# A graph network on sparse lists: the stage that builds the lists, from the scheduler's order to an order written by hand

## The chip, the core and the metric

The kernel runs on one core of a Trainium2 chip, in one launch. The metric is the device time of that launch in microseconds (us). A core has five engines that work at once, each with its own in-order queue of instructions: TensorE (PE; its weight loads are shown as PEld), VectorE (DVE), ScalarE (ACT), GpSimd (POOL) and SyncE (SP). SP only starts DMAs here; POOL also starts the gathers. Semaphores order the engines among each other.

## What is computed

Two residual layers of graph attention on 4096 nodes of 512 features. The adjacency is a 4096 x 4096 matrix of zeros and ones whose density falls with both the row and the column number, so that the first rows have many neighbours and the later ones few. Cut to what matters:

```python
x = layernorm(x + gat0(x, adj, W, a))                # 8 heads of 64
def gat(x, adj, W, a):                               # per head
    h = x @ W
    e = leaky_relu(h @ a_dst + (h @ a_src)[None], 0.2)   # N x N
    e = where(adj > 0, e, -inf)
    return softmax(e) @ h
h1 = elu(gat(x, adj, W1, a1))                        # 8 heads of 64
h2 = elu(gat(h1, adj, Wo, ao))                       # 1 head of 512
x = layernorm(x + relu(h2 @ lin1_w + lin1_b) @ lin2_w + lin2_b)
```

## The kernel before, in words

The kernel never forms the N x N scores. In a first stage, the graph stage, it turns each tile of 128 rows of the adjacency into a list of edges (source node in `idx`, target row in `nl`), 128 edges to a chunk, 927 chunks in all. Three attention layers then gather the projected rows of the listed nodes from a table in memory and sum them. If a list did not fit its room, a flag would start a dense path that is not run with these inputs. The change is in the graph stage alone, which `find_edges` issues and which also computes the first projection.

There are 35 lists. Rows 0 to 127 (tile 0) have so many edges that they make four lists, by column ranges; tiles 1 to 31 make one each. `parts()` gives for each list the room per row `k`, the number of chunks `n` and the segments of columns within which at most 8 (tile 0: 24) neighbours are looked for. A list goes this way:

- SP loads the adjacency rows (`raw`, int32), ACT turns them into bf16 zeros and ones (`sg`), and PE adds a multiple of the column number to each edge by two matmuls per 512 columns (`key`, in PSUM, two buffers of 1024 columns).
- DVE takes the eight largest keys of each segment (`cand`, MAX8; for tile 0 three rounds with a replacement between), then the `k` largest of the candidates (`lst`) in rounds of MAX8 and MATCH_REPLACE8. Each round needs the one before it.
- ACT makes column numbers of them (`qs`) and the row's degree (`signs`, `balance`); POOL makes `degs` and `counts`.
- PE sums the counts over the rows (`prs`, one PSUM bank). ACT makes from it where each row starts and ends and compares that with a ramp (`starts`, `ends`, `sides`), and POOL adds the two halves into `s1`, the matrix that spreads rows over edges. ACT and POOL split the columns into two bf16 parts (`rhs`, `rest`).
- PE multiplies `s1` with those parts (`pl`, one PSUM bank, in up to four pieces); ACT copies `nl`; DVE picks each edge's column (`sel`, `src`); POOL writes `hole` and `idx`.

Beside it, for each of 32 node tiles, `x` is loaded (`xr`), turned by PE (`pt`), copied by ACT (`xt`), multiplied with the weights in two halves of eight fp32 matmuls in all (two passes each, `ph`), and copied into a row of the table (`hrow`), which SP writes. `load_projection` loads the weights of a layer and adds columns `w @ a` to them: POOL multiplies (`sprod`), DVE sums.

In the code the lists come by tile number. `places_of` delays the second half of a list's way (`place`) by one list, and `beside(t)` issues one projection after each tile. But this stage is not under `tc.manual_schedule()`: a scheduler takes the instructions and orders each engine's queue anew, by its own idea of costs. The attention layers that follow are under `manual_schedule` and keep the order in which the code issues them. Their first gathers wait for the whole table and for `idx`.

Of the kernel before, what the change touches and what calls it, by code (L numbers as in the profile page):

```python
# [10 lines left out]
F32 = mybir.dt.float32  # L11
# [547 lines left out]
def sparse_path(  # L559
# [84 lines left out]
    def load_projection(pool, st, w, a):  # L644

        hs, dm = st.heads, st.dim


        st.w = pool.tile([P, FC, 2, st.wide], F32, name=f"sw_{st.name}")
        for c in range(FC):  # L650
            for j in range(2):
                mine = st.w[:, c, j, :HF]
                if hs > 1:
                    nc.sync.dma_start(
                        mine.rearrange("p (k o) -> p k o", o=dm),
                        w[ts(j, hs // 2), ts(c, P), :].rearrange("k f o -> f k o"),
                    )
                else:
                    nc.sync.dma_start(mine, w[0, ts(c, P), ts(j, HF)])
        with tc.tile_pool(name=f"swload_{st.name}", bufs=2) as wp:  # L660
            for side in range(2):
                ab = wp.tile([P, hs, dm], F32, name="sab")
                nc.sync.dma_start(ab, a[:, ts(side, dm)].partition_broadcast(P))
                d = (side == 1) == st.dest_first
                for c in range(FC):
                    prod = wp.tile([P, 2, HF], F32, name="sprod")
                    nc.gpsimd.tensor_mul(  # L667
                        prod, st.w[:, c, :, :HF], ab.rearrange("p h d -> p (h d)").rearrange("p (j f) -> p j f", j=2)
                    )
                    if hs > 1:  # L670
                        at = HF if d else HF + hs // 2
                        nc.vector.tensor_reduce(
                            st.w[:, c, :, at : at + hs // 2],
                            prod.rearrange("p j (h d) -> p j h d", d=dm), AX.X, OP.add,
                        )
                    else:
                        nc.vector.tensor_reduce(st.w[:, c, int(d), HF:], prod, AX.XY, OP.add)
# [12 lines left out]

    def project_in(ps, st, columns, n=P):

        halves = []
        for j in range(2):
            ph = ps.tile([P, st.wide], F32, name="ph")
            for c in range(FC):
                nc.tensor.matmul(ph[:n], columns(c), st.w[:, c, j], start=(c == 0), stop=(c == FC - 1))  # L697
            halves.append(ph)
        return halves
# [73 lines left out]
    def edge_constants(big):  # L773
# [64 lines left out]
        return frac, places, iota_e, iota_k, row1, own_b, before, values, mids, ends_at, by_parts  # L838

    def signs_of(sb, t, pieces=1):  # L840

        raw = sb.tile([P, N], I32, name="raw", bufs=2)
        sg = sb.tile([P, N], BF16, name="sg")
        w = N // pieces
        for i in range(pieces):
            nc.sync.dma_start(raw[:, ts(i, w)], adj[ts(t, P), ts(i, w)])
        for i in range(pieces):
            nc.scalar.activation(sg[:, ts(i, w)], raw[:, ts(i, w)], AF.Sign)  # L848
        return sg

    def find_edges(big, sb, ps, pk, constants, sg, beside):

        frac, places, iota_e, iota_k, row1, own_b, before, (less, under), mids, ends_at, by_parts = constants
# [8 lines left out]
        places_of = []  # L864
        for v, p in enumerate(pts):
            t, k, c0, nch = p.t, p.k, p.first, p.n
            if t > 0:
                sg = signs_of(sb, t)
            size = sum(8 * r for _, _, r in p.segs)
            cand = sb.tile([P, size], F32, name="cand", bufs=1 if t == 0 else 2, tag="cand0" if t == 0 else "cand")  # L870
            at = 0
            for w0_ in range(p.lo // 1024 * 1024, p.hi, 1024):
                a, b = max(w0_, p.lo), min(w0_ + 1024, p.hi)
                key = pk.tile([P, 1024], F32, name="key")
                for j in [a] + list(range((a // KW + 1) * KW, b, KW)):
                    e, w = min(b, (j // KW + 1) * KW), j // KW
                    out_ = key[:, j - w0_ : e - w0_]
                    nc.tensor.matmul(out_, ident_b, sg[:, j:e], start=True, stop=False)  # L878
                    nc.tensor.matmul(out_, places[:, w], frac[:, j - w * KW : e - w * KW], start=False, stop=True)  # L879
                for j, n, r in p.segs:  # L880
                    if not a <= j < b:
                        continue
                    part = key[:, j - w0_ : j - w0_ + n]
                    for i in range(r):
                        nc.vector.max(out=cand[:, at : at + 8], in_=part)  # L885
                        if i < r - 1:
                            left = sb.tile([P, 256], F32, name="left")[:, :n]
                            nc.vector.match_replace(
                                out=left, in_to_replace=cand[:, at : at + 8], in_values=part, imm_value=-1.0
                            )  # L890
                            part = left
                        at += 8

            r8 = 8 * p.segs[0][2]
            skip = sum(n <= r8 for _, n, _ in p.segs)
            last = cand.rearrange("p (s e) -> p s e", e=r8)[:, skip:, r8 - 1]
            nc.vector.tensor_reduce(over[:, 0, v : v + 1], last, AX.X, OP.max)
            lst = sb.tile([P, kmax], F32, name="lst")[:, :k]
            for i in range(k // 8):
                nc.vector.max(out=lst[:, ts(i, 8)], in_=cand)  # L900
                if i < k // 8 - 1:
                    nc.vector.match_replace(  # L902
                        out=cand, in_to_replace=lst[:, ts(i, 8)], in_values=cand, imm_value=-1.0
                    )

            qs = sb.tile([P, kmax + 1], F32, name="qs")[:, : k + 1]
# [13 lines left out]
            if p.last:  # L920
                mean = sb.tile([P, 3], F32, name="mean_of")
                nc.gpsimd.tensor_scalar(mean[:, 0:1], sum_, 0.5, None, op0=OP.is_lt)
                nc.gpsimd.tensor_scalar(mean[:, 1:2], sum_, 0.5, None, op0=OP.is_gt)
# [3 lines left out]
                nc.gpsimd.tensor_add(counts[:, v : v + 1], deg, mean[:, 0:1])  # L927
            else:
                nc.gpsimd.tensor_copy(counts[:, v : v + 1], deg)
            deg = counts[:, v : v + 1]  # L930
            def place(v=v, p=p, k=k, c0=c0, nch=nch, qs=qs, deg=deg):
                prs = ps.tile([P, 1], F32, name="prs", tag="small")
                nc.tensor.matmul(prs, before, deg, start=True, stop=True)
                nc.scalar.activation(qs[:, k:], prs, AF.Identity, bias=ends_at[:, v : v + 1], scale=-1.0)

                lim = sb.tile([P, 1], F32, name="lim")
                nc.gpsimd.tensor_sub(lim, deg, mids[:, v : v + 1])
                first = starts[:, v : v + 1]
                nc.scalar.activation(first, prs, AF.Identity, bias=mids[:, v : v + 1], scale=-1.0)
                nc.scalar.activation(ends[:, v : v + 1], prs, AF.Identity, bias=lim)  # L940
                wide = p.blocks * P
                here = s1[:, p.at * P : p.at * P + wide]
                sides = sb.tile([P, 2, most * P], BF16, name="sides")[:, :, :wide]
                nc.scalar.activation(sides[:, 0], iota_e[:, :wide], AF.Sign, bias=first)
                nc.scalar.activation(sides[:, 1], iota_e[:, :wide], AF.Sign, bias=ends[:, v : v + 1], scale=-1.0)  # L945
                nc.gpsimd.tensor_add(here, sides[:, 0], sides[:, 1])  # L946


                rhs = sb.tile([P, 2 * (kmax + 2)], BF16, name="rhs")[:, : 2 * (k + 2)].rearrange("p (h w) -> p h w", h=2)
                rest = sb.tile([P, 2 * (kmax + 1)], BF16, name="rest")[:, : 2 * (k + 1)].rearrange("p (h w) -> p h w", h=2)  # L950
                q2 = sb.tile([P, 2 * (kmax + 1)], F32, name="q2")[:, : 2 * (k + 1)].rearrange("p (h w) -> p h w", h=2)
                shape = [P, 2, k + 1]
                for h in range(2):
                    nc.scalar.activation(rhs[:, h, : k + 1], qs, AF.Copy, scale=half[:, h : h + 1])
                nc.gpsimd.tensor_mul(q2, qs[:, None, :].to_broadcast(shape), half[:, :, None].to_broadcast(shape))
# [44 lines left out]
            if len(places_of) > 1:  # L1000
                places_of.pop(0)()
# [629 lines left out]
```

## Time and profile before

| | us |
|---|---|
| three runs | 2115.8, 2120.51, 2120.89 (median 2120.51) |
| span of the profiled execution, first to last instruction | 2110.3 |
| time around the span, against the median | 10.2 |
| first gather of the first layer (end of the graph stage) | 489.4 |
| busy in 0 to 490: PE, DVE, ACT, POOL | 345.0, 367.1, 294.7, 215.1 |
| busy in the whole span: PE, DVE, ACT, POOL | 1707.7, 1323.1, 663.4, 1155.6 |

The page shows no device time of its own for the profiled execution; its span is compared with spans, and times with times. Busy time is the time in which at least one instruction of the engine ran. Matmuls are pipelined and their shown ends are modelled, so PE's busy time is more than it needs. "A <- B" in a view means that A stood idle until B was done. In a row of the timeline the first number is the start in us from the span's start, the second the duration, and a bracket at the end is the idle time ahead of it and what ended that.

### The profile page before, as it was taken

What the parts mean: (1) busy time and instruction counts of PE and PEld (TensorE: products, weight loads), DVE (VectorE), ACT (ScalarE), POOL (GpSimd) and SP (SyncE); (2) the same over time, 40 slices, a digit from 0 to 9 for tenths busy, and PEclk for the clock granted to TensorE, in tenths of its full rate; (3) what the DMA queues carried; (4) which work ended last, traced back from release to release, by engine and by line L of the source; (5) the groups of instructions that cost most, each with busy time, mean ns of one, the idle gap of its engine ahead of it and who ended that gap; (6) DMA issues with size and microseconds to landing.
All of it is one profiled execution on the core that took longest, in us unless ns stands there. A gap on an engine that the chain in (4) does not pass through costs nothing.

```text
span 2110.3 us, 29302 instructions
## 1 busy us (share of the span) xinstructions
PE 1707.7 (81%) x8987; PEld 999.2 (47%) x8987; DVE 1323.1 (63%) x3933; ACT 663.4 (31%) x2316; POOL 1155.6 (55%) x1658
## 2 busy tenths in 40 slices
PE   4778777663888887848888988579999989998997
PEld 3555443221555565525555665354454444444444
DVE  6887777774899998947878878433433333433412
ACT  3447677664222222202333332121110212111111
POOL 5515444446777777737777777373647444443200
PEclk9899999775899999978999999889999999999999
DMA  7434566634777888737777777373546343534301
GB/s 230 150 101 161 210 259 226 224 145 131 231 234 230 252 238 241 208 87 195 185 189 191 194 200 192 123 223 91 158 119 185 110 127 91 156 103 122 97 13 47
DMA packets 132589, 351.94 MB, mean 167 GB/s; under 512 B 41922, under 2 KB 42954, under 8 KB 128454
## 3 DMA queue, kind: packets, MB, share of 16 engines
q0 software_dynamic: 74160, 206.25, 36.0%
q1 hardware_dynamic: 58262, 143.72, 19.3%
q8 instruction: 74, 1.21, 0.2%
q14 instruction: 93, 0.76, 0.1%
HBM read 347.31 MB, written 42.24 MB: 185 GB/s over the span
## 4 chain that ended last, share of the span: by engine, by line
PE 34%; DVE 19%; issue 15%; POOL 13%; DMA 12%; ACT 6%; SPq 1%; POOLq 0%; DVEq 0%; ACTq 0%
PE acc L1230 11%; PE p L1508 10%; DMA g<-table_t,idx 10%; POOL g L1094 9%; PE ph L697 5%; DVE g L1218 5%; PE p L1520 4%; DVE cand L885 2%; DMA xr<-sx_d 1%; DVE cand L902 1%; POOL s L946 1%; DVE lst L900 1%; ACT sides L945 1%; POOL sprod L667 1%; DVE sm L1197 1%
## 5 line engine op out<-in xcount | busy, mean ns | idle before, releaser
L1094 POOL DMA_INDIRECT g<-table_t,idx x927 | 941.1, 1015 | 552.9 <-issue 232.8
L1230 PE MATMUL acc<-g,sm 128*64 128x260 f32 (+2 forms) x4068 | 580.8, 415 | 175.1 <-DVE g L1218 141.8
L1230 PEld LDWEIGHTS acc<-g,sm 128*64 128x64 f32 x4068 | 328.3, 147 | 391.8 <-DVE g L1218 156.8
L697 PE MATMUL ph<-sw_t,xt 128*128 128x264 f32 (+1 forms) x1536 | 394.0, 404 | 51.5 <-ACT xt L686 51.3
L1218 DVE TENSOR_TENSOR g<-g,wp 128x2048 f32<-128x2048 f32 (+4 forms) x134 | 349.1, 2605 | 6.7 <-ACT wp L1173 6.7
L697 PEld LDWEIGHTS ph<-sw_t,xt 128*128 128x128 f32 x1536 | 291.9, 197 | 120.0 <-ACT xt L686 72.3
L885 DVE MAX8 cand<-key 128x8 f32<-128x353 f32 (+55 forms) x467 | 195.1, 445 | 74.6 <-PE key L879 74.4
L1508 PE MATMUL p<-sht,sl1w 128*128 128x512 f32 (+1 forms) x576 | 228.7, 553 | 0.7 <-DVE xr L1525 0.7
L1520 PE MATMUL p<-sl2w,shid 128*128 128x512 f32 x512 | 226.7, 597 | 0.0
L686 ACT ACTIVATE xt<-pt 128x128 f32<-128x128 f32 x384 | 101.3, 279 | 216.0 <-PE pt L683 215.8
L1508 PEld LDWEIGHTS p<-sht,sl1w 128*128 128x128 f32 x576 | 107.8, 191 | 111.5 <-issue 106.0
L1520 PEld LDWEIGHTS p<-sl2w,shid 128*128 128x128 f32 x512 | 95.2, 190 | 119.9 <-issue 119.4
L1165 DVE TENSOR_TENSOR z<-s,g 128x16 f32<-128x16 f32 (+9 forms) x294 | 46.6, 175 | 138.0 <-DMA g<-table_t,idx 134.9
L878 PE MATMUL key<-sg,s_identb 128*128 128x512 bf16 (+1 forms) x258 | 109.7, 426 | 20.6 <-DVE cand L885 11.1
L1511 ACT ACTIVATE shid<-p,sl1b 128x512 f32<-128x512 f32 (+1 forms) x72 | 46.1, 640 | 242.9 <-PE p L1508 242.9
L1267 DVE SCALAR_TENSOR_TENSOR o<-ex,o 128x512 f32<-128x512 f32 x64 | 44.2, 691 | 124.5 <-ACT ex L1266 124.3
L848 ACT ACTIVATE sg<-raw 128x4096 bf16<-128x4096 int32 (+1 forms) x39 | 116.9, 2996 | 8.9 <-PE key L878 5.2
L710 ACT COPY hrow<-ph 128x260 f32<-128x260 f32 (+2 forms) x194 | 71.0, 374 | 148.8 <-PE ph L697 148.4
L879 PE MATMUL key<-frac,places 128*128 128x512 bf16 (+1 forms) x258 | 109.4, 425 | 2.7 <-POOL places L784 2.7
L1205 DVE TENSOR_SCALAR sm<-iota_n,nl,w 128x64 f32<-128x64 f32 x339 | 83.8, 327 | 30.8 <-ACT w L1176 30.8
L1173 ACT ACTIVATE wp<-z 128x32 f32<-128x32 f32 (+4 forms) x134 | 27.5, 205 | 207.0 <-DVE g L1218 206.5
L1525 DVE TENSOR_TENSOR xr<-p,xr 128x512 f32<-128x512 f32 x32 | 22.0, 688 | 94.1 <-PE p L1520 93.6
(184 smaller groups left out, 1836.8 us busy)
## 6 DMA issues: line engine op xcount, KB each, us to landing
raw<-in_adj_dram SPq DMA_DIRECT2D x31, 2048.0 KB, 7.9
table_t<-hrow SPq DMA_DIRECT2D x64, 260.0 KB, 3.6
xr<-in_x_dram SPq DMA_DIRECT2D x64, 256.0 KB, 4.0
g<-table_t,idx POOLq DMA_INDIRECT x927, 3.8
table_t<-hrow SPq DMA_DIRECT2D x32, 257.0 KB, 4.3
sx_d<-o SPq DMA_DIRECT2D x32, 256.0 KB, 4.6
xr<-sx_d SPq DMA_DIRECT2D x32, 256.0 KB, 4.0
out_dram<-xr SPq DMA_DIRECT2D x32, 256.0 KB, 3.4
```

Of the source, the lines that this page charges most:

```text
L686: nc.scalar.activation(xt[:, c, :], pt[:, c, :], AF.Copy, accum_out=st.xparts[:, c, t : t + 1])
L697: nc.tensor.matmul(ph[:n], columns(c), st.w[:, c, j], start=(c == 0), stop=(c == FC - 1))
L848: nc.scalar.activation(sg[:, ts(i, w)], raw[:, ts(i, w)], AF.Sign)
L878: nc.tensor.matmul(out_, ident_b, sg[:, j:e], start=True, stop=False)
L879: nc.tensor.matmul(out_, places[:, w], frac[:, j - w * KW : e - w * KW], start=False, stop=True)
L885: nc.vector.max(out=cand[:, at : at + 8], in_=part)
L1094: nc.gpsimd.indirect_dma_start(out=u.g[:, k, : self.st.row], out_offset=None, in_=self.st.table[:, :], in_offset=bass.IndirectOffsetOnAxis ...
L1205: nc.vector.tensor_scalar(sm[:, at + i], of_g, node[k], u.w[:, k], op0=OP.is_equal, op1=OP.mult)
L1218: nc.vector.tensor_mul(body, body, wp[:, :, :, None].to_broadcast(body.shape))
L1230: nc.tensor.matmul(out_[g * HN : (g + 1) * HN], sm[:, slot], rows(k), start=start, stop=stop)
L1508: nc.tensor.matmul(p1, l1w[:, c, ts(k, P)], hts[b][:, c, :n], start=(c == 0), stop=(c == FC - 1))
L1520: nc.tensor.matmul(p2, hids[b][:, k, ts(j, P)], l2w[:, k, :], start=(k == 0), stop=(k == HC - 1))
```

## The change

The graph stage gets `tc.manual_schedule()`, and its order is written out:

- A `Clock` counts DVE's time by formulas (`tick`). Steps are put on it with a delay (`later`) and are issued when the count passes their time. `idle` holds work for PE that is issued only while a counter `spare` is positive: it grows with DVE's time and shrinks with PE's work.
- A list's way is cut into `front`, `middle`, `back` and `pick`, each given to the clock by the one before it.
- Lists come by turns: one of the last tile, then one heavy list (tiles 0 to 7) and two light ones from the end.
- The adjacency is loaded and signed in halves of 2048 columns, four buffers each. A load is issued when an earlier half is signed; signs are issued up to four windows of 1024 columns ahead of their use. The very first halves come in four and two pieces.
- Keys of the window after next are issued as soon as DVE is through with a window.
- A projection is three pieces of idle work: the turn and two halves. `load_projection` becomes a generator that gives one product at a time; the weights of the first layer are loaded after the first adjacency halves and multiplied after the first list. Those of the later layers come at lists 14 and 24.
- Some buffers change: `qs`, `rhs`, `rest` three instead of two, `sides`, `sel` and `sab` one instead of two.

The diff, cut to its core:

```diff
+    class Clock:
+        def __init__(self):
+            self.now, self.due, self.count, self.spare, self.idle = 0.0, [], 0, 0.0, []
+        def later(self, delay, fn, *args):
+            self.count += 1
+            heapq.heappush(self.due, (self.now + delay, self.count, fn, args))
+        def tick(self, cost):
+            end = self.now + cost
+            self.spare = min(self.spare + cost, 3.0)
+            while True:
+                if self.due and self.due[0][0] <= end:
...
+                elif self.idle and self.spare > 0 and self.idle[0][0] <= end:
...
+        def drain(self):
+            while self.due or self.idle:
+                self.spare = 1.0
+                self.tick(1.0)
...
+        heavy = [v for v, p in enumerate(pts) if p.t < 8]
+        light = [v for v, p in reversed(list(enumerate(pts))) if p.t >= 8]
+        turns_ = [light.pop(0)]
+        while heavy or light:
+            turns_ += heavy[:1] + light[:2]
+            heavy, light = heavy[1:], light[2:]
...
+        def sign(t, h, pieces=1):
+            raw = raws.pop((t, h))
+            name, bufs = ("sg0", 2) if t == 0 else ("sg", 4)
+            sg = sgs[t, h] = sb.tile([P, HW], BF16, name=name, bufs=bufs)
+            w = HW // pieces
+            for i in range(pieces):
+                nc.scalar.activation(sg[:, ts(i, w)], raw[:, ts(i, w)], AF.Sign)
+            if stream:
+                load(*stream.pop(0))
...
+            clock.later(2.2, middle, v, qs, lim)
+        def middle(v, qs, lim):
...
+            for lo in range(0, p.n, per):
+                clock.later(1.8 + 4.5e-3 * wide, queue, v, rhs, rest, lo, per)
...
+            clock.later(1.6, pick, v, lo, per, pl, kk)
...
+        for j in range(4):
+            load(*stream.pop(0), *cuts[j : j + 1])
+        for j in range(2):
+            sign(*signed.pop(0)[1:], cuts[j])
+        between(-1)
...
+        fill(0)
+        fill(1)
+        for n, v in enumerate(turns_):
...
+            while i < len(windows) and windows[i][0] == v:
...
+                        nc.vector.max(out=cand[:, at : at + 8], in_=part)
+                        tick(0.09 + n_ / 960)
...
+                fill(i + 2)
+                i += 1
+                while signed and signed[0][0] <= i + 3:
+                    sign(*signed.pop(0)[1:])
...
+            front(v, lst)
+            between(n)
+        clock.drain()
...
-        sg0 = signs_of(sb, 0, 8)
-        constants = edge_constants(big)
...
+        pools.enter_context(tc.manual_schedule())
+        constants = edge_constants(big)
+        clock = Clock()
...
+        def turn0(t):
+            xt = turn_in(sb, pp, st0, xrs.pop(t), t)
+            ask0(t + 2)
+            clock.idle.append((clock.now + 2.0, 1.95, half0, (t, xt, 0)))
+        def half0(t, xt, j):
+            ph = project_half(pp, st0, lambda c: xt[:, c, :], j)
+            clock.later(1.5, out0, t, ph, j)
+            if j == 0:
+                clock.idle.append((clock.now + 0.5, 1.95, half0, (t, xt, 1)))
...
+        def between(n):
+            if n < 0:
+                clock.w0 = load_projection(big, sb, st0, w0, a0)
+                first = next(clock.w0)
+                clock.w0 = itertools.chain([first], clock.w0)
+            if n == 0:
+                weigh(clock.w0)
+                clock.later(11.0, ask0, 0)
+                clock.later(11.0, ask0, 1)
+                clock.idle.append((clock.now + 14.0, 0.95, turn0, (0,)))
+            if n == 14:
+                gap[0] = 4.0
+                weigh(load_projection(late, sb, st1, w1, a1))
+            if n == 24:
+                weigh(load_projection(late, sb, st2, wo, ao))
```

## The prediction

> **What bounds the kernel now.** The change touches one stage, so the first question is how long that stage is and what stands still in it. The instructions on `idx` give its end: the layers' first gather starts at 489.4 us of a span of 2110.3. The busy time by stretches says which engine is full up to there; its columns are busy us of PE, PEld, DVE, ACT, POOL with counts in brackets, then granted clock, DMA share, GB/s.
>
> ```profile
> L1094 POOL DMA_INDIRECT g<-table_t,idx x927: 996/1002/1602, 489.4 to 1979.9; - x186
> ```
>
> ```profile
> 300.00:350.00 50.00, 36.82 (x198) 19.48 (x196) 37.79 (x128) 38.03 (x98) 21.19 (x82) 1.00 0.63 229
> ...
> 450.00:490.00 40.00, 21.73 (x109) 9.07 (x107) 26.01 (x89) 19.97 (x49) 17.16 (x68) 0.71 0.06 20
> 0.00:490.00 490.00, 344.97 (x1751) 201.10 (x1751) 367.12 (x1417) 294.74 (x843) 215.10 (x732) 0.89 0.52 184
> ```
>
> No engine is full: DVE, the busiest, works 367 of 490 us. The table of waits within the stage says why: every engine waits for another one's step of a list's way.
>
> ```profile
> DVE cand L885 <- PE key L879: 74.4, 55, 5.7
> ...
> PE prs L933 <- POOL counts L927: 36.0, 29, 3.1
> ...
> PE pl L969 <- POOL s L946: 32.9, 30, 2.1
> ```
>
> The timeline of one light list shows the mechanism. PE reaches the product on `s1` before POOL has made it and stands; the key matmuls for the next list are queued behind; DVE waits for those.
>
> ```profile
> 317.18 0.20 PE L969 MATMUL pl<-rhs,s 128*128 128x52 bf16 x1 [1.66 <-POOL s L946]
> ...
> 318.64 0.22 DVE L885 MAX8 cand<-key 128x8 f32<-128x53 f32 x1 [1.79 <-PE key L879]
> ```
>
> Such a list takes 9.4 us (its `sides` start at 305.19, the next list's at 314.55), of which DVE works 7.1. So the stage is bound by latency in PE's queue, and DVE's own time is what it could shrink to. One more reading decides how far. An instruction of DVE that needs the result of the one just ahead starts after its end; one that needs something older starts before it:
>
> ```profile
> 28.95 0.34 DVE L902 MATCH_REPLACE8 cand<-lst,cand 128x192 f32<-128x192 f32 x1
> 29.33 0.36 DVE L900 MAX8 lst<-cand 128x8 f32<-128x192 f32 x1
> ...
> 461.03 0.44 DVE L885 MAX8 cand<-key 128x8 f32<-128x274 f32 x1
> 461.39 0.22 DVE L900 MAX8 lst<-cand 128x8 f32<-128x72 f32 x1
> ```
>
> 29.33 lies 0.04 after 28.95 + 0.34; 461.39 lies 0.08 before 461.03 + 0.44. Over the stage, 983 of DVE's 1408 neighbouring pairs overlap by 0.083 and 107 stand tight at +0.035: the planner has put another list's work between most dependent steps.
>
> [...] 512-wide key matmuls are 0.43 apart at 459.55 and 0.22 apart elsewhere, with a clock of 0.71 in the last stretch. [...] a sign takes 0.63 for 512 columns and 3.60 for 4096, which leaves 0.2 fixed.
>
> **The change part by part**, S being the time that DVE stands between its first maximum and the end of the last list.
>
> 1. *DVE in hand order: the floor.* The same maxima, replacements and selections are issued (467 + 78 + 161 MAX8, 204 replacements with their value loads, 35 triples and 51 fused selections). But a list's rounds now follow one another with nothing between: the changed program has 498 tight pairs, mostly maximum, replacement, maximum. The durations of all DVE instructions of the stage sum to 448.8. Pairs: 204 value loads overlap by 0.014, 51 accumulator reads by 0.076, 498 stand at +0.035, 655 overlap by 0.083: 448.8 - 2.9 - 3.9 + 17.4 - 54.4 = 405. The same sum for before gives 367, what the table shows. So the hand order costs DVE 38 us, which nothing hides once DVE is the full engine.
> 2. *Start.* The first maximum waits for POOL's `places`, as before (8.32); I take 8.5. The first weights come later: SP now issues eight pieces of adjacency, then two loads that wait until ACT has signed list 31's halves (about 7.6 and 11.6), and only then the eight weight DMAs (6.85 for eight) and the row of `a` (2.63 to land): 11.6 + 6.9 + 0.5 + 2.6 = 21.6 behind 6 MB of adjacency, so some 23. DVE meets the first sum over `sprod` near 18.5 and waits for a product of 1.26: 5 us of S, 1 more for list 31's second half. POOL stands there too, with list 31's `s1` and PE's `pl` behind it.
> 3. *The way in four steps.* `prs` is issued 2.2 us of DVE work after the list, `pl` another 1.8 + 4.5e-3 x width, the selection 1.6 after that. The chain needs about 0.65 on ACT, 0.75 on POOL and 0.4 on PE (1.8); then 0.5 + 1.3 on ACT and 1.2 + 0.3 on POOL (3.3, against 4.1 given at width 512). So PE's waits mostly go, and the 74 us of DVE waiting for keys. What is late next is ACT.
> 4. *Halves on ACT.* 68 signs in place of 39: 62 of 2048 columns at 0.63 + 1536 x 0.83 ns = 1.90, two of 1024 at 1.05, four of 0.63, together 122.4 against 116.9: +5.5. In a light list ACT works 38.03/50 x 9.4 = 7.1 now, 7.3 then; DVE 7.1 plus some seven pairs that become tight at 0.12, about 7.9. ACT at 93% in strict order, with waits for `prs` and `pl` in its queue, will hold DVE up; I take 0.3 for each of 24 light lists, 7 us. The pieces' added DMAs (29 at about 0.33 of SP) lie two tiles ahead, beside other work.
> 5. *Selections and keys.* 50 selections wait for ACT's copy of `pl`: 0.2 to 0.3 each, 12. Keys behind a half projection (8 matmuls at 0.27, 2.15): 3. These are estimates from the waits before (DVE behind `nl` and `kk` 23 us in 15 waits), nearest row; the bounds are 0 and those 23, doubled.
> 6. *Light and heavy by turns.* One heavy and two light lists ask 6 to 7.5 MB in about 36 us, 210 GB/s at most, against 258 seen at 250 to 300; no wait added.
> 7. *Projections between.* PE's sum is 111 (keys), 155 (32 projections of 0.5 + 16 x 0.27), about 35 for the rest: it has room. But five of the 32 stand behind the last key matmul in PE's queue. Each is 0.5 of transposes, 1.3 until ACT's copy, 4.3 of matmuls: 5 x 6.1 less the first one's 1.8, 29; two `pl` 1; then `split_s` 2.2, the mean row's matmuls 2.1, copies 0.8, its DMA 3.6, about 40 us from the last key matmul to the first gather. Before it was 489.4 - 475.3 = 14.
>
> Sum: the last key matmul comes two windows and one list's rounds (2.4 + 0.2 + 2.3) ahead of DVE's end of the last list. That end is 8.5 + 405 - 1 (the cast ahead) - 7 (selections, split and verdict after it) + S = 405.5 + S. So the first gather is at 405.5 - 4.9 + 40 + S, about **441 + S**, against 489.4: gain 48 - S. With S = 6 + 7 + 12 + 3 = 28 the gain is **20 us**. The layers keep their program. The page gives the profiled execution's span, 2110.3; the median of the three timed runs is 2120.51, 10.2 of it outside that span. I carry that over: span 2090, time 2100.5.
>
> **The rivals.**
> - *A (0.54), as summed:* S between 18 and 42, 2091 to 2114.
> - *B (0.19), the chain is hidden nearly whole:* for it speaks that PE and POOL are far from full; against it ACT's 93%. S of 8 to 18 leaves a gain of 30 to 40: 2081 to 2091, centre 2086.
> - *C (0.15), ACT becomes the bound, and it is slower:* signs, `prs` readers and projection copies in one strict queue; a sign waiting 1.5 us for `prs` delays the key fill that DVE needs next. It decides from S = 48, that is, if a light list takes over 8.7 instead of 8.2 and the selections wait 0.5 each. At 1.0 per light list and 0.6 per selection S = 6 + 24 + 30 + 3 = 63: 15 us slower, 2136. For it speaks that hand order can't step past a late step, against it the time given in step 3.
> - *D (0.12), it doesn't do what it says:* the tight pairs (38) and the late projections (26) take back the removed waits; S of 42 to 54, within 6 us of before.
>
> About 0.3% (6 us) is what a measurement of this kernel can tell from no change. Faster by more: A and B, 0.73; within: D, 0.12; slower by more: C, 0.15. Range: S from 8 (no less than start and one short wait in ten) to 53: 2081 to 2126.
>
> **What would show it.** First gather near 469; DVE's busy time in the stage near 405 instead of 367 with the same durations; DVE waiting for keys well under 74 and for `nl`, `kk` and `sprod` more than before; a tail of some 35 to 40 us in which PE does projections while DVE is nearly idle. Wrong: DVE still at 367 (the pairs don't stand apart), a tail under 20, or light lists over 9 us.

## The result, and the profile after

The changed kernel is slower. Its median is 2141.1 us (four runs, 2138.0 to 2147.2) against 2118.2 for the kernel before (four runs, 2115.7 to 2120.9): ratio 1.0112, 95% interval 1.0089 to 1.0136. The forecast was 2100.5 with a range up to 2126.

Three readings give the place. The instructions on `idx` first: the first gather of the layers.

```profile
L1240 POOL DMA_INDIRECT g<-table_t,idx x927: 992/998/1595, 515.2 to 2014.5; - x186
```

It starts at 515.2, 25.8 us later than before (489.4) and 46 later than forecast (469). So the loss is in the graph stage. The layers, whose program is the same, take 1620.9 from the first gather to the end before and 1630.2 after; in the later profiles of this study, all with the same layers, that stretch varies from 1621.9 to 1629.7. The profiled execution of after is also the slowest of its four. So below, the first gather is used for the stage, medians for times.

The busy time by stretches comes second (columns as in the prediction: PE, PEld, DVE, ACT, POOL, then granted clock, DMA share, GB/s).

```profile
20.00:60.00 40.00, 16.96 (x55) 8.99 (x57) 27.10 (x108) 10.93 (x40) 16.52 (x31) 0.60 0.48 157
...
250.00:300.00 50.00, 29.26 (x150) 15.86 (x151) 33.53 (x103) 24.65 (x58) 23.30 (x63) 0.70 0.58 172
300.00:350.00 50.00, 34.86 (x194) 19.09 (x198) 42.12 (x136) 36.32 (x90) 27.22 (x82) 0.84 0.66 220
350.00:400.00 50.00, 32.25 (x151) 17.72 (x153) 34.92 (x110) 29.06 (x75) 20.51 (x67) 0.74 0.68 224
...
450.00:490.00 40.00, 32.05 (x178) 19.94 (x181) 33.59 (x107) 31.27 (x96) 22.07 (x78) 0.96 0.36 120
```

Where the order runs as meant, DVE works 42 of 50 us (300 to 350; before 38). But there are holes, 20 to 60, 250 to 300 and 350 to 400, where PE, DVE, ACT and POOL all work less and PE's granted clock is 0.60, 0.70 and 0.74. The waits of DVE within the stage name what ends them.

```profile
DVE cand L1123 <- PE key L957: 32.1, 28, 7.0
DVE sw_t L674 <- POOL sprod L665: 24.2, 4, 10.7
...
DVE sel L1063 <- ACT nl L1046: 8.7, 6, 6.2
DVE sw_t L679 <- POOL sprod L665: 8.5, 2, 8.0
DVE sel L1071 <- ACT kk L1051: 5.7, 4, 2.3
```

Keys fell from 74 us to 32, as forecast in direction. The longest wait for `nl`, 6.2, lies behind the last list. The sums over `sprod`, 13 us before, are now 33 in six waits. Three of these make up most of it: 10.7 at the start, 10.6 at list 14 and 8.0 at list 24. The one at list 14 can be followed over three queues. DVE's timeline:

```profile
260.72 1.30 DVE L1123 MAX8 cand<-key 128x8 f32<-128x768 f32 x2 [0.73 <-PE key L957]
272.65 0.69 DVE L674 TENSOR_REDUCE sw_t<-sprod 128x8 f32<-128x512 f32 x1 [10.63 <-POOL sprod L665]
```

POOL's:

```profile
271.36 1.26 POOL L665 TENSOR_TENSOR sprod<-sw_t,sab 128x512 f32<-128x512 f32 x1 [8.79 <-DMA sab<-in_a_dram]
```

And SP's queue of DMA issues:

```profile
250.06 9.91 SPq L934 DMA_DIRECT2D raw<-in_adj_dram  x2
260.02 6.29 SPq L656 DMA_DIRECT2D sw_t<-in_w_dram  x8
266.40 0.45 SPq L683 DMA_DIRECT2D sab<-in_a_dram  x1
...
268.33 21.51 SPq L934 DMA_DIRECT2D raw<-in_adj_dram  x3
289.94 0.38 SPq L683 DMA_DIRECT2D sab<-in_a_dram  x1
```

Read upwards: SP stands 9.9 us in two adjacency loads, whose buffers come free only when ACT has signed an earlier half; eight weight DMAs and the row of `a` stand behind them in SP's queue; POOL's product waits 8.8 for the row; DVE's sum waits 10.6 for the product, and the maxima, whose keys are long there, stand behind the sum. The second row of `a` then waits behind three more loads (21.5).

What the forecast had right is in the rounds of a list. Before, another list's maximum lay between most dependent steps; now there is none:

```profile
481.45 0.28 DVE L1145 MAX8 lst<-cand 128x8 f32<-128x120 f32 x1
481.76 0.09 DVE L1147 MATCH_VALUE_LOAD cand<-lst,cand 128x8 f32 x1
481.84 0.27 DVE L1147 MATCH_REPLACE8 cand<-lst,cand 128x120 f32<-128x120 f32 x1
482.14 0.29 DVE L1145 MAX8 lst<-cand 128x8 f32<-128x120 f32 x1
```

482.14 lies 0.03 after 481.84 + 0.27. The late projections are also where they were put: key matmuls end at 479.96, and five projections of 16 matmul records each (two to a matmul) and the mean row follow until 512.

```profile
479.58 0.38 PE L957 MATMUL key<-frac,places 128*128 128x512 bf16 x1
479.79 3.72 PE L703 MATMUL ph<-sw_t,xt 128*128 128x264 f32 x16
...
500.29 3.83 PE L703 MATMUL ph<-sw_t,xt 128*128 128x264 f32 x16 [0.52 <-ACT xt L694]
...
506.63 5.18 PE L703 MATMUL ph<-sw_t,mean 128*1 128x264 f32 x16 [0.23 <-DVE mean L759]
```

The stage adds up: first maximum 9.6, DVE without waits 403.9, waits (S) 70.3, which is 483.8, the end of the last list; less 3.9 to the last key matmul, plus a tail of 35.3: 515.2.

### The profile page after: what moved, and what is told of

Read it like the earlier page. It is cut to its first block, busy times and chain, and to the rows that moved or that the text cites. A ratio compares the mean times of both kernels' runs of the same rounds, so it can differ in the third digit from the quotient of the medians.

```text
span 2145.5 us, 29380 instructions
## 1 busy us (share of the span) xinstructions
PE 1715.8 (80%) x8960; PEld 1011.4 (47%) x8987; DVE 1353.1 (63%) x3934; ACT 666.2 (31%) x2345; POOL 1154.7 (54%) x1657
## 3 DMA queue, kind: packets, MB, share of 16 engines
q0 software_dynamic: 74160, 206.25, 35.4%
q1 hardware_dynamic: 62438, 143.72, 19.9%
## 4 chain that ended last, share of the span: by engine, by line
PE 28%; DMA 13%; DVE 13%; issue 12%; POOL 8%; ACT 2%; POOLq 0%; SPq 0%; DVEq 0%; ACTq 0%
DMA g<-table_t,idx 11%; PE acc L1376 10%; PE p L1700 10%; POOL g L1240 8%; DVE g L1364 4%; PE ph L703 4%; PE p L1712 3%; DMA xr<-sx_d 1%; DVE sm L1343 1%; DVE bs L1417 1%; DVE z L1311 1%; DVE sm L1351 1%; DVE z L1312 1%; DVE o L1396 1%; PE pt L691 1%
## 5 line engine op out<-in xcount | busy, mean ns | idle before, releaser
L1376 PE MATMUL acc<-g,sm 128*64 128x260 f32 (+2 forms) x4068 | 588.2, 419 | 175.0 <-DVE g L1364 140.2
L703 PE MATMUL ph<-sw_t,xt 128*128 128x264 f32 (+1 forms) x1536 | 383.2, 402 | 36.7 <-ACT xt L694 33.1
L1123 DVE MAX8 cand<-key 128x8 f32<-128x92 f32 (+57 forms) x467 | 179.0, 442 | 32.2 <-PE key L957 32.1
L943 ACT ACTIVATE sg<-raw 128x2048 bf16<-128x2048 int32 (+2 forms) x68 | 123.0, 1809 | 7.6 <-DMA raw<-in_adj_dram 7.5
L1319 ACT ACTIVATE wp<-z 128x32 f32<-128x32 f32 (+4 forms) x134 | 27.5, 205 | 209.1 <-DVE g L1364 208.7
L956 PEld LDWEIGHTS <-s_identb 128*128 128x128 bf16 x258 | 29.5, 114 | 113.0 <-issue 47.2
```

Source lines behind the costliest of these rows:

```text
L956: nc.tensor.matmul(out_, ident_b, sg[:, j % HW : j % HW + e - j], start=True, stop=False)
L1376: nc.tensor.matmul(out_[g * HN : (g + 1) * HN], sm[:, slot], rows(k), start=start, stop=stop)
```

## The experiments

All are edits of the changed kernel; none leaves work out. The table gives the median, the ratio to runs of the kernel before taken beside it with its interval (a surer comparison than that of two medians), and from the profile the first gather, the tail behind the last key matmul, DVE's time without waits between its first maximum and the end of the last list, and its waits there (S) by what they are for. A tight pair, below, is two neighbouring instructions of DVE of which the second starts just after the first has ended (by 0.03 us in the rows above), since it needs its result. S counts gaps of 0.06 us and more; the wait of 7 ahead of the first maximum is not in it.

| kernel | median | ratio to before | first gather | tail | DVE without waits | S: keys + sprod + rest |
|---|---|---|---|---|---|---|
| before | 2118 | 1 | 489.4 | 13.8 | 365.9 | 68.8 + 13.4 + 22.7 |
| after | 2141.1 | 1.0112 (1.0089 to 1.0136) | 515.2 | 35.3 | 403.9 | 25.1 + 32.7 + 12.5 |
| e1_weights | 2121.8 | 1.0034 (1.0019 to 1.0048) | 496.8 | 36.2 | 403.8 | 20.4 + 17.6 + 13.0 |
| e2_tail | 2143.7 | 1.0137 (1.0118 to 1.0157) | 518.1 | 14.6 | 410.1 | 47.3 + 25.0 + 15.4 |
| e4_pairs | 2128.2 | 1.0061 (1.0044 to 1.0078) | 498.9 | 35.9 | 387.0 | 21.2 + 32.8 + 16.2 |
| e6_all | 2131.0 | 1.0079 (1.0063 to 1.0096) | 503.2 | 14.5 | 393.6 | 56.2 + 13.8 + 19.3 |
| e7b_late | 2139.7 | 1.0104 (1.0070 to 1.0138) | 511.2 | 39.8 | 404.7 | 20.6 + 31.3 + 9.0 |
| e8b_best | 2112.0 | 0.9972 (0.9958 to 0.9987) | 488.0 | 41.5 | 390.0 | 25.2 + 10.8 + 14.7 |
| e9b_lists | 2117.8 | 0.9999 (0.9989 to 1.0009) | 493.5 | 48.3 | 368.5 | 20.1 + 16.0 + 35.4 |
| e10b_quarters | 2151.2 | 1.0156 (1.0133 to 1.0180) | 522.1 | 14.5 | 406.9 | 47.4 + 27.5 + 19.9 |
| e13_mid | 2099.1 | 0.9909 (0.9885 to 0.9933) | 469.8 | 14.5 | 392.5 | 30.0 + 10.1 + 16.9 |
| e3_whole | 2147.3 | 1.0126 (1.0098 to 1.0153) | 519.9 | 33.8 | 405.7 | 27.5 + 29.2 + 17.9 |
| e3_in_order | 2129.5 | 1.0052 (1.0034 to 1.0071) | 504.2 | 44.8 | 405.8 | 13.1 + 20.9 + 13.9 |
| e12_planner | 2085.2 | 0.9839 (0.9815 to 0.9863) | 459.5 | 16.9 | 354.5 | 52.2 + 10.5 + 22.0 |
| e15_pl_order | 2106.9 | 0.9951 (0.9933 to 0.9968) | 479.3 | 15.9 | 363.8 | 59.6 + 9.8 + 26.3 |
| e16_pl_whole | 2090.1 | 0.9872 (0.9847 to 0.9896) | 463.8 | 17.5 | 354.4 | 51.1 + 13.3 + 23.6 |
| e17_pl_early | 2094.0 | 0.9886 (0.9861 to 0.9910) | 469.1 | 17.3 | 354.5 | 55.8 + 3.8 + 34.7 |

**e1_weights: is it the queue ahead of the weights?**

```diff
-                weigh(load_projection(late, sb, st1, w1, a1))
+                weigh(clock.w1)
...
+            if n == 10:
+                clock.w1 = ahead(late, sb, st1, w1, a1)
+            if n == 20:
+                clock.w2 = ahead(late, sb, st2, wo, ao)
...
+        between(-1)
         for j in range(2):
             sign(*signed.pop(0)[1:], cuts[j])
-        between(-1)
```

> Changed kernel with the weights asked for ahead of the adjacency in SP's queue at the start, and at lists 10 and 20 for the products of lists 14 and 24; both rows of a at once. Theory (DVE stands behind POOL's products, and these behind loads that SP reaches only after adjacency loads that wait for ACT's signs): DVE's waits for sprod fall from 33 us to under 6, the first gather from 515 to 482 to 490, the time by 25 to 33 us, to about the time of the kernel before. Rival (ACT is the full engine, the weights only show where DVE stands): the waits move to keys, nl and kk, first gather over 505 and less than 10 us gained. Rival 2 (the DMA rate at the start is what is short): then the first maxima and keys come later by what the weights take, 6 to 10 us, and half the gain goes.

The first gather came at 496.8, 18.4 earlier than in after, and the ratio fell from 1.0112 to 1.0034, which is 17 us. At lists 14 and 24 the theory holds: of 20.8 us of waits for `sprod` 3.8 are left. The edit does two things there, asking earlier and asking for both rows of `a` at once; how much each gives was not separated. At the start it fails, where the wait grew from 11.9 to 13.8 (waits of DVE in e1_weights):

```profile
DVE sw_t L674 <- POOL sprod L665: 17.1, 3, 13.8
```

It was not the weights that were late there. By the trace's semaphore records the first row of `a` had landed at 21.8 us, against 27.9 in after. POOL stood for a step of the first list, which its queue has ahead of the product:

```profile
29.16 0.19 POOL L972 TENSOR_SCALAR degs<-balance 128x1 f32<-128x1 f32 x1 [11.02 <-ACT signs L970]
...
31.08 2.50 POOL L665 TENSOR_TENSOR sprod<-sw_t,sab 128x512 f32<-128x512 f32 x2
```

And ACT came to `signs` late, because a sign ahead of it in ACT's queue had to wait for its half of the adjacency:

```profile
26.56 1.91 ACT L946 ACTIVATE sg<-raw 128x2048 bf16<-128x2048 int32 x1 [8.69 <-DMA raw<-in_adj_dram]
28.38 0.30 ACT L967 ACTIVATE qs<-lst,value 128x24 f32<-128x24 f32 x1
28.58 0.30 ACT L970 ACTIVATE signs<-lst,value 128x24 f32<-128x24 f32 x1
```

SP issued that half at 18.69, behind the weights; in after it was issued at 8.71, ahead of them, and its sign started at 18.13. So rival 2 comes nearest, though by another way: the first maximum is not later (9.64 in both), but what the weights gained a later half lost, 8.4 us. The busy time of e1_weights from 2 to 35 us, the last three columns being PE's clock, the DMA share and GB/s:

```profile
2.00:35.00 33.00, 8.63 (x26) 2.90 (x27) 11.30 (x44) 13.03 (x20) 20.20 (x101) 0.75 0.98 336
```

The DMA engines are busy 0.98 of that time (after: 0.93), which leaves little room to bring both sooner, as an estimate from that share.

**e7b_late: meeting the first sums later.**

```diff
-                weigh(clock.w0)
-                clock.later(11.0, ask0, 0)
-                clock.later(11.0, ask0, 1)
-                clock.idle.append((clock.now + 14.0, 0.95, turn0, (0,)))
+                clock.later(16.0, weigh, clock.w0)
+                clock.later(24.0, ask0, 0)
+                clock.later(24.0, ask0, 1)
+                clock.idle.append((clock.now + 28.0, 0.95, turn0, (0,)))
```

> Changed kernel with the first layer's products, sums and projections given out 13 to 16 us later; loads and their order in SP's queue stay. Theory (the 11.9 us at the start are DVE meeting the sums before weights that the saturated DMA engines cannot bring sooner): the wait for sprod before 60 us goes from 11.9 to under 2, the first gather from 515 to 503 to 506, the time down by 9 to 12. Rival (what is given out later is missed at the end): two more projections stand behind the last key, the tail grows from 35 to 43 or more, and the first gather stays over 510.

Both sides a little right: the waits for the first layer's sums went from 11.9 to 10.9, in five of 0.9 to 3.5. The first products now come at 38.7 and have steps of two lists between them in POOL's queue; and one of them waits 4.6 for the second row of `a`, which, with one buffer, is asked for only at 48.9. DVE reached the last key 8.6 earlier, the tail grew by 4.6, and the first gather came 4 earlier. In time it cannot be told from after.

**e4_pairs: the price of a tight pair.**

```diff
+                for two in zip(todo[::2], todo[1::2] + [iter(())] * (len(todo) % 2)):
+                    for _ in itertools.zip_longest(*two):
+                        pass
```

> Changed kernel with the rounds of two neighbouring segments of tile 0's lists issued by turns (maximum a, maximum b, replacement a, replacement b), nothing else. Theory (a dependent neighbour starts 0.035 after the end, an independent one 0.083 before it): some 130 to 150 tight pairs less, DVE's time without waits in the stage 404 to 386 to 389, first gather 515 to 497 to 501, time down by 14 to 18 us. Rival (DVE runs ahead only into waits for weights, keys and ACT): time without waits falls as said, but the waits grow by as much, and the first gather stays over 508.

As the theory said: 332 tight pairs in place of 468, DVE without waits 387.0 in place of 403.9, that is 0.124 us for each of 136, and the waits stayed (70.2). The first gather came 16.3 earlier, and the ratio fell by 0.0051, 11 us. This is the forecast's floor measured by itself.

**e2_tail and e10b_quarters: can PE take the late projections earlier?**

```diff
-            clock.idle.append((clock.now + 2.0, 1.95, half0, (t, xt, 0)))
+            clock.idle.append((clock.now + 2.0, 1.2, half0, (t, xt, 0)))
...
-                clock.idle.append((clock.now, 0.95, turn0, (t + 1,)))
+                clock.idle.append((clock.now, 0.3, turn0, (t + 1,)))
```

> Changed kernel with the prices lowered at which a projection is let in between (0.95 to 0.3 for the turn, 1.95 to 1.2 for a half), so that fewer projections are left behind the last key matmul. Theory (the tail of 35 us is late projections, and PE has room for them earlier): tail from last key matmul to first gather 35 to about 15 to 20, first gather 515 to 497 to 502, time down by 13 to 18 us. Rival (PE is short of room: a half projection more ahead of the keys makes DVE wait): DVE's waits for keys grow from 25 to 35 or more, and the first gather stays over 508.

> The kernel with the lower prices (e2_tail) with each half projection's four products issued as two pairs with room for key matmuls between them. Theory (keys wait because four products of about 0.5 us stand ahead of them in PE's queue): DVE's waits for keys go from 47 us (e2_tail) back to 25 to 32, the tail stays near 15 to 20, first gather 518 to 498 to 505. Rival (PE has not the time, whatever the pieces: its clock is low and the projections' 155 us and more have to be paid somewhere): waits for keys stay over 42, first gather over 510.

The rival of e2_tail was right: the tail lost 20.7 and the keys gained 22.2. Cutting a half in two pieces did not help (keys 47.4, and no faster). PE's timeline in e10b_quarters shows why this run does not settle whether short pieces would help:

```profile
119.60 0.38 PE L957 MATMUL key<-frac,places 128*128 128x512 bf16 x1
119.81 3.63 PE L1568 MATMUL ph<-sw_t,xt 128*128 128x264 f32 x8
123.25 0.32 PE L995 MATMUL prs<-counts,before 128*128 128x1 f32 x2
123.42 1.14 PE L1568 MATMUL ph<-sw_t,xt 128*128 128x264 f32 x4
124.40 0.38 PE L956 MATMUL key<-sg,s_identb 128*128 128x512 bf16 x1
```

Three pieces stand one behind the other, ahead of the next keys, since `spare` had been saved up; DVE stood 4.15 us for those keys at 125.46. That is the size of the block again, not of the piece.

**e6_all: e1, e2 and e4 together.**

> The three edits together: weights asked for ahead, lower prices for projections, rounds of tile 0's lists by turns of two. Theory (three separate costs of the changed kernel: waits for weights 29, tail 15 to 18, tight pairs 15 to 18): first gather 515 to 452 to 462, time about 2080 to 2090, some 30 to 40 us faster than the kernel before. Rival (one engine, ACT or PE, is near full, and DVE's gain turns into waits for it): first gather 470 to 485, time no better than the kernel before by more than 10 us.

503.2, later than even the rival allowed: keys cost DVE 56.2. That the prices are too low for what a projection takes fits this; e13_mid, below, raises them.

**e8b_best, e13_mid, e9b_lists: the three repairs, with three settings around them.** e8b_best has the late first weights (both rows of `a` at once), the early others, and the rounds by turns; e13_mid has prices of 0.6 and 1.6 in addition; e9b_lists, on the prices of e8b_best, puts the rounds that sort `lst` between the next list's maxima:

```diff
-            for q in range(k // 8):
-                nc.vector.max(out=lst[:, ts(q, 8)], in_=cand)
...
+                    for _ in itertools.zip_longest(*two):
+                        next(rest, None)
...
+            rest = finish(n, v, k, size, cand)
```

> Changed kernel with the later start of the first layer's weights, the other two layers' weights asked for four lists ahead, and tile 0's rounds by turns of two. Theory (separate costs of 12, 19 and 17): first gather 515 to 466 to 471, waits for sprod under 5, time 2092 to 2098, faster than the kernel before by about 20. Rival (the wait only changes its name, as with the lower prices): first gather 485 or later and no faster than the kernel before.

> The kernel with three edits (e8b_best) with prices between the changed kernel's and the lower ones (0.6 for a turn, 1.6 for a half). Theory (PE's projections cost DVE as much in waits for keys as they take from the tail): tail 41 to 25 to 32, waits for keys 25 to 33 to 40, first gather within 5 us of 488. Rival (there is room between, only the lowest prices pass it): waits for keys grow by less than half of what the tail loses, first gather 473 to 482, time about 2100.

> The edits of the kernel with three of them (late first weights, early other weights, tile 0's rounds by turns), and also the rounds that sort a list's candidates issued one by one between the next list's maxima (the front of the list's way after its last round). Theory (tight pairs cost 0.12 each): some 250 tight pairs less than the some 330 left, DVE's time without waits from 387 to 357 to 362, first gather some 25 us before that of the kernel with three edits, time about 2070. Rival (DVE's slack is what hides the list's way; with none, keys, prs readers and copies wait again as in the kernel before, where DVE's time was 366 and its waits 105): DVE's time falls as said and its waits grow by 20 or more, first gather within 8 us of the kernel with three edits.

e8b_best gained 27 of the forecast 46: waits for `sprod` were 10.8 and not under 5, and the tail grew from 35.3 to 41.5, since projections start later. The first gather is where the rival put it, but the kernel is just faster than the one before. In e13_mid the tail then went from 41.5 to 14.5 for 4.8 more of keys: its rival was right, there is room on PE. (e2's lower prices were not run on this base; in e6_all, the nearest to it, keys took 56.2.) That 469.8 is within 1 us of the prediction's first gather is chance: S is 57.0 here, not 28, and the tail 14.5, not 40. In e9b_lists DVE without waits is 368.5, as low as before, but waits for `nl` and `kk` rose by 20 and the tail by 7; its rival was right.

**e3_whole and e3_in_order: two parts of the change undone.**

```diff
-    HW = N // 2
+    HW = N
...
-        turns_ = [light.pop(0)]
-        while heavy or light:
+        turns_ = list(range(nv))
```

> Changed kernel with the adjacency loaded and signed in whole tiles again (buffers of the same bytes: two whole ones in place of four halves), all else as changed. The prediction's step 4 gave the halves 7 us on ACT: then the first gather goes from 515 to about 508. Its rival C (ACT as the full engine, signs in its strict queue) gives more: 505 or earlier. Theory now (ACT has slack, and the loads wait for signs, the weights for loads): a sign of 3.6 in place of 1.9 stands ahead of the prs readers, DVE's waits for ACT and for sprod stay or grow, first gather 515 to 530, time the same or up to 15 us longer.

> Changed kernel with the lists in their first order (tile 0's and the other heavy ones first, the light ones after them) in place of heavy and light by turns. Theory (heavy lists have the room on PE for projections, light ones ask 2 MB each 8 to 9 us): projections are nearly all done ahead, tail 35 to about 15; in the light stretch DVE waits for keys and signs, 45 to 60 us in place of 25, and the first gather is at 505 to 525. Rival (turns matter for DMA alone and DMA is not short): waits for keys stay under 30 and the first gather falls to 490 to 500.

Whole tiles are not faster (1.0126 against 1.0112, intervals overlap): the 7 us that step 4 put on halves do not come back when the halves go, and rival C's bound on ACT does not show either. Lists in their first order are 12 us faster under the written order, which neither side has whole: keys fell to 13.1, as the rival said, and `sprod` to 20.9, but the tail was 44.8 and not 15, and the first gather, 504.2, is later than the rival's.

**e12_planner: the written order undone, all else kept.**

```diff
-        pools.enter_context(tc.manual_schedule())
```

> Changed kernel with one line less: the graph stage is not held to the written order, the planner orders each engine again, over the new program (halves, turns, four steps). Theory (the planner puts other lists' work between dependent steps, and puts the sums over sprod where their data is there): tight pairs 468 to under 200, DVE's time without waits 404 to 365 to 380, waits for sprod 33 to under 15, waits for keys and ACT more than with the written order, first gather 480 to 500, time 2105 to 2125. Rival (the order of buffers binds the planner to the written order): tight pairs over 350, first gather over 505.

Better than expected: 2085.2, 1.6% faster than the kernel before. Its instructions on `idx`:

```profile
L1240 POOL DMA_INDIRECT g<-table_t,idx x927: 992/998/1594, 459.5 to 1957.3; - x186
```

55.7 us earlier than after, by one line. DVE's timeline shows what the line had cost:

```profile
425.78 0.26 DVE L1145 MAX8 lst<-cand 128x8 f32<-128x104 f32 x1
425.95 0.23 DVE L1123 MAX8 cand<-key 128x8 f32<-128x85 f32 x1
426.10 0.07 DVE L1147 MATCH_VALUE_LOAD cand<-lst,cand 128x8 f32 x1
426.16 0.25 DVE L1147 MATCH_REPLACE8 cand<-lst,cand 128x104 f32<-128x104 f32 x1
426.33 0.29 DVE L1123 MAX8 cand<-key 128x8 f32<-128x137 f32 x1
```

A maximum of the next list lies between the steps, and each next row starts before the one ahead of it has ended (425.95 against 425.78 + 0.26). Against after: DVE without waits -49.4 (50 tight pairs in place of 468), tail -18.4, waits +14.4, the lead of the last key -2.0, the first maximum -0.3: -55.7. The waits are in other places (waits of DVE in e12_planner):

```profile
DVE cand L1123 <- PE key L957: 58.7, 44, 6.8
...
DVE sel L1071 <- ACT kk L1051: 14.6, 8, 4.4
DVE sw_t L674 <- POOL sprod L665: 6.5, 7, 3.4
```

**e15_pl_order, e16_pl_whole, e17_pl_early: which other part gains, under the planner.** Each is e12_planner with one edit: first order of the lists, whole tiles, or the later weights asked for four lists ahead.

> The planner's version of the changed kernel (e12_planner) with the lists in their first order in place of heavy and light by turns. Theory (turns level PE and DMA: light lists alone ask 2 MB of adjacency and five busy us of PE each 8 to 9 us, so in the kernel before the light stretch stood in latency): first gather 459 to 475 to 490, DVE's waits for keys grow by 15 or more, time 2100 to 2116. Rival (turns are worth nothing or cost, as under the written order, where taking them away gained 11): first gather 450 to 462, time 2075 to 2088.

> The planner's version with adjacency loaded and signed in whole tiles. Theory (a sign of 3.6 in ACT's queue and a whole load before its sign make keys late; halves let both start earlier): DVE's waits for keys 59 to 65 to 80, first gather 459 to 465 to 480, time 2090 to 2105. Rival (halves only cost ACT 5.5): first gather 452 to 460, time 2078 to 2086.

> The planner's version with the second and third layers' weights asked for four lists ahead. Theory (the planner has already put the sums where their data is there; 10 us of waits for sprod are left, of which 5 are of these lists): first gather within 4 us of 459, time 2080 to 2088. Rival (the wait behind adjacency loads is still paid in other engines): first gather 448 to 454, time 2072 to 2079.

Heavy and light by turns are worth 19.8 us of the stage and 1% of the time (0.9951 against 0.9839, intervals apart). The theory had that size, but not its parts: waits for keys grew by 7.4 and not 15, and DVE's time without waits by 9.3. Halves are worth 5 us by the medians, which the intervals do not tell apart, and waits for keys did not grow without them. e15_pl_order, which keeps the halves, the new steps and the buffers but not the turns, is 10 us below the kernel before; what of that each gives was not separated. e17_pl_early fits neither side: `sprod` fell by 6.7, but waits for `kk` rose by 12 and the first gather came 9.7 later. Why an earlier load makes another step late under the planner was not followed up.

## Why the prediction was wrong, step by step

- **The formula held, and its term S did not.** First gather = 441 + S; with the measured S of 70.3 it gives 511 against 515.2. S had been put at 28. Of the 42.3 us that are missing, 20.8 are waits for the products of the later layers' weights, which the prediction put at nothing without a reason; 15.1 are keys, and 5.9 the start.
- **Step 1 (floor) was right.** 397 forecast (405, less a cast and the work after the list), 403.9 measured, tight pairs 468 against 498; the price of a pair, what a dependent one costs DVE more than an independent one, came out at 0.124 us by e4_pairs against 0.118. The 38 us were in the sum. What the prediction did not weigh is the new program under the planner, which pays almost none of them (50 tight pairs in e12_planner).
- **Step 2 (start): 6 forecast, 11.9 measured.** The queue was read rightly; what failed is the time of the data. The eight weight DMAs took SP 10.0 to issue and not 6.9, and the row of `a` 5.8 from its issue to POOL's start and not 2.6, with the DMA engines busy 0.93 of the time from 2 to 35 us. So the first product, put at some 23, ran at 28.0. e1_weights shows that asking sooner only moves the delay to the adjacency (a half 8.4 later).
- **Step 2's mechanism, not carried on: 0 forecast, 20.8 measured. This is the step that failed most.** The same queue stands ahead of the weights of lists 14 and 24, but the prediction followed the DMAs of a moved step through SP's queue at the start only. e1_weights took 17.0 of this out and 17 us off the time; so that part is shown, for the earlier request and both rows at once together.
- **Steps 4 and 5 (halves and keys): 10 forecast, 25.1 measured.** e3_whole shows that the halves are not the cause. By PE's trace, projections ran in four of these waits, 8.9 us in all; in waits of 9.7 us PE ran nothing but key matmuls, and in the other 6.5 also `prs` or `pl`. So the blocks of projections that e10b_quarters shows are a third here at most. PE's clock may be another part: from 37.70, ahead of which PE had stood 5.3 us, key matmuls are 0.43 apart at a granted clock of 0.50 (37.6 to 39.6), and at 479.36 they are 0.22 apart at 1.00 (478.9 to 479.8). In before, too, they are 0.43 apart in more places than at 459.55, as from 449.61 to 451.74. No run here separates that share or shows what lowers the clock, and the cause of the rest stays open.
- **Step 5 (selections): 12 forecast, 8.7 measured** behind `nl` and `kk`. The mechanism was not the one summed: not 50 waits of 0.2 to 0.3, but nine of 0.15 to 2.3. That the size is near is luck.
- **Step 6 (turns at nothing) was wrong both ways:** a cost of 12 us under the written order, a gain of 20 under the planner. Why the sign turns is argued, not shown: under the written order the turns cost 12.0 at keys and 11.8 at `sprod` (32.7 against 20.9, perhaps because the later weights fall among more adjacency loads), and the tail gave 9.5 back.
- **Step 7 (tail): 40 forecast, 35.3 measured.** Five late projections as counted. Two sizes in it were off and partly cancel: projections followed each other after 5.1 on average and not 6.1, and the mean row's matmuls took 5.2 and not 2.1. What the step did not ask is whether they had to be late: e13_mid, at 2099.1, shows that they had not.
- **The time around the span:** 10.2 was carried over from a profiled execution of before and a median of others. After's profiled run took 2147.2 with a span of 2145.5, so 1.7 lies around it; later runs of the kernel before lie 2.2 to 2.5 outside their spans. So the profile of before was most likely an execution below the median (estimate: 2110.3 + 2.4, some 2113). It matters little, since both sides are compared by medians, but the level of the forecast rested on it.

Rival C ended on the right side for another reason: it had ACT as the bound, and DVE's waits behind ACT's copies did not grow as it needed. S passed C's threshold of 48 through `sprod`, with SP's queue as the cause, and through keys. As for where the expected gain went: the 44 us of waits for keys that the written order did remove (68.8 to 25.1) were more than taken back: 38.0 more of DVE's own time, 21.5 in the tail and 19.3 of `sprod`.

## What to carry to other kernels

The order written by hand took 44 us of waits for keys away here and put new ones where an instruction sat ahead of its data (19.3 us more for `sprod`), so follow each DMA of every moved step through the issuing queue at every place, not at the first one. When a change brings a new program and a new order together, try the new program under the old scheduler first: here that one line was worth 56 us. Work that a scheduler puts between dependent short steps was worth 0.12 us per pair here (e4_pairs), and a count of pairs in the compiled order prices it before anything runs.

## What the runs showed of the hardware that was not expected

Two things. At the start of the stage the DMA engines are busy 0.93 (after) to 0.98 (e1_weights) of the time from 2 to 35 us. Asking for the weights 7.5 us sooner there (issue from 4.6 in place of 12.1) brought them sooner (the first row of `a` at 21.8 in place of 27.9), but an adjacency half 8.4 later, and through two in-order queues (ACT stood 8.69 for the half, POOL 11.02 for ACT's `signs`) the product that needs the weights came later too, at 31.1 in place of 28.0. And in after PE and DVE waited for each other with neither full: of the first 490 us they were busy 323.1 and 390.0, and DVE stood 32.1 for keys. PE's waits for DVE, in after:

```profile
PE key L956 <- DVE cand L1123: 78.1, 40, 10.4
```

and in e12_planner:

```profile
PE key L956 <- DVE cand L1123: 7.7, 10, 1.9
```

With two key buffers and the written order PE stood 78 us for a buffer; under the planner it stood 8 for the same buffers, and 35 for `counts` instead.
